# Moving a residual kernel's twelve data slots to the front of SBUF, at a multiple of 4096 bytes

## The chip, the cores and the metric

The kernel runs on one core of a Trainium2 chip. The metric is device time in microseconds (us) for one execution. Three runs of the kernel before took 325.68 to 326.02 us, with a median of 325.93 us. Times of single instructions and of stretches come from one profiled execution of the same kernel.

## The reference

There are 128 samples. Each has a matrix of 128 channels by 1024 time steps, and an index that names one of 8 subjects. Each subject has a 128 x 128 weight matrix. The output is the input plus the input multiplied by its subject's weights, all in float32:

```python
def reference(x, itok_B_0_7, L0_cond_weights):
    # x (128, 128, 1024), itok_B_0_7 (128,), L0_cond_weights (8, 128, 128)
    w = L0_cond_weights[itok_B_0_7]
    return x + jnp.einsum("bct,bcd->bdt", x, w)
```

One sample is 512 KB, so 67.1 MB are read and 67.1 MB are written, beside 0.5 MB of weights.

## The kernel before

The 128 samples are treated in 32 tiles of four samples, and a tile in two halves of two samples (`G = 2`, `H = 2`). A tile lives in one of 12 slots `x0` to `x11` in SBUF (line 95). A slot has 16384 bytes in each of the 128 partitions, four rows of 4096 bytes, one row for each sample. Tile `i` uses slot `i % 12`. A sample is loaded into its row, the sum is written over it, and the row is stored from there.

Loads are issued on ScalarE's queue, one of 512 KB for each sample (`load`, line 128). On the side of the input, four channels at a time form one run of 16384 bytes (`ROWS = 4`); on the side of SBUF, each channel is a row of 4096 bytes in its own partition. From the thirteenth tile on, ScalarE waits until the tile that had the slot has been stored.

Stores are issued on SyncE's queue (`store`, line 137), as a rule one of 2 MB for each tile, after both halves are summed. On the side of SBUF a run is the two neighbouring rows of a half, 8192 bytes; on the side of the output it is one row of 4096 bytes. Sample 0 goes by itself: it has its own load semaphore, product, sum and store, and so does sample 1 after it (line 229 on, `if j == 0`); their stores are 512 KB each, with runs of 4096 bytes. The second half of tile 0 and the first half of the last tile are stored as 1 MB, and the last two samples by themselves.

For each half tile `j`, GpSimd reads the subjects' indices, waits until the half has been loaded and copies the two subjects' weights from `w_all` into two of four buffers `ws` (line 210). TensorE then multiplies, four matmuls of 512 columns for each sample in two passes (line 223), into one of two PSUM tiles. VectorE adds the product to the slot's rows (line 242, and line 235 for sample 0). Before the first product TensorE multiplies zeros three times (line 155).

All of this is written in a fixed order for each engine; no planner decides it. The addresses of the tiles follow the order in which `sbuf(...)` is called (lines 89 to 95): first the four index rows, then all weights, the four weight buffers and the zeros, and the 12 slots last. What the language sets aside at the start of each partition ends at byte 16512. So the index rows begin there, and slot 0 at 26752.

Of the kernel before, what the change touches and what calls it, by code (L numbers as in the profile page):

```python
# [30 lines left out]
G = 2  # L31
H = 2
# [3 lines left out]
SLOTS = 12  # L36
# [8 lines left out]

ROWS = 4

PACE = 2
QUEUES = {mybir.EngineType.SP: "qSPDynamicHW", mybir.EngineType.Activation: "qActDynamicHW"}

# [22 lines left out]
def kernel(  # L73
# [7 lines left out]
    nc = tc.nc  # L81
    B, C, T = x.shape
# [3 lines left out]
    def sbuf(name, *shape, dtype=F32):  # L86
        return ctx.enter_context(nc.sbuf_tensor(name, list(shape), dtype)).ap()

    given, near, wrap, index = (
        sbuf(name, 1, B, dtype=I32) for name in ("given", "near", "wrap", "index")  # L90
    )
    w_all = sbuf("w_all", C, S, D)
    ws = [sbuf(f"w{i}", C, 1, D) for i in range(W_SLOTS)]
    zeros = sbuf("zeros", C, N)
    xs = [sbuf(f"x{i}", C, H * G, T) for i in range(SLOTS)]
    ps = [
        ctx.enter_context(nc.psum_tensor(f"ps{i}", [D, G, T], F32)).ap() for i in range(P_SLOTS)
    ]
# [19 lines left out]
    def emptied(i, h):  # L118

        turns = i // SLOTS  # L120
        return (DMA * G + (DMA if h == H - 1 else 0)) * turns - (DMA if i >= SLOTS and i % SLOTS == 0 and h == 0 else 0)
# [26 lines left out]
    with tc.tile_critical():  # L148
# [22 lines left out]
        for i in range(NT):  # L171
# [4 lines left out]
            if i >= SLOTS:  # L176
                nc.scalar.wait_ge(s_pair[k][H - 1], emptied(i, H - 1))
            if i == PACE:
                nc.scalar.wait_ge(s_one_issued, 1)
# [4 lines left out]
        for j in range(NT * H):  # L184
            i, q0, q1 = j // H, j % H * G, (j % H + 1) * G
# [105 lines left out]
```

## Time and profile before

| | |
|---|---|
| median of three runs | 325.93 us (325.68 to 326.02) |
| profiled execution | 325.98 us |
| its span, first to last instruction | 324.2 us |
| mean granted TensorE clock | 0.925 |
| TensorE matmul busy | 241.9 us (75%) |
| VectorE busy | 148.0 us (46%) |
| GpSimd busy | 34.3 us (11%) |
| moved by DMA | 134.85 MB in 16218 packets, mean 416 GB/s |
| load of one sample, issue to landing | 32.1 us (median of 128) |
| store of one tile, issue to landing | 47.0 us (median of 30) |

The span runs from the first instruction to the last; what the execution takes beyond it, 1.8 us here, lies around it. Busy shares are means over the span. DMA issues are not counted as busy time of the engine that issues them. A packet in the DMA rows is one run on the reading side, or a 4-byte write to a semaphore; 16 DMA engines work at the same time, and shares are of their time together.

### The profile page before, as it was taken

To read this page: it belongs to the slowest core of one execution; us is meant where nothing else is said; L and a number is where in the kernel's file an instruction comes from. 1 tells how busy PE (TensorE), PEld (TensorE's weight loads), DVE (VectorE), ACT (ScalarE), POOL (GpSimd) and SP (SyncE) were. 2 spreads that over 40 slices of the span, in tenths; PEclk is the share of its full clock that TensorE was granted. 3 is DMA by queue.
4 is the path that set the end of the run, shared out by engine and by line. 5 is a ranking of instruction groups with operands and counts; after the bars stand their busy time and mean duration, and the time that the engine had idled before them with its cause. 6 is when DMAs were issued, how large, how long until landed. Compare 5 with 4: busy or idle time off the path is not lost.

```text
span 324.2 us, 1611 instructions
## 1 busy us (share of the span) xinstructions
PE 241.9 (75%) x518; PEld 94.9 (29%) x518; DVE 148.0 (46%) x69; POOL 34.3 (11%) x132
## 2 busy tenths in 40 slices
PE   7999888888888888898888888888888769000000
PEld 3444333333333333333333333333333324000000
DVE  1566554555555554555555555555554552200000
POOL 1011110111111111111111111111111010000000
PEclk9999999999999999999999999999999997755555
DMA  7999999999999999999999999999999999999996
GB/s 259 395 427 429 422 425 423 427 428 424 427 426 425 426 418 430 427 420 432 423 422 426 424 426 421 428 422 426 428 428 419 424 428 424 427 423 429 427 427 255
DMA packets 16218, 134.85 MB, mean 416 GB/s; under 512 B 2641, under 2 KB 3666, under 8 KB 4178
## 3 DMA queue, kind: packets, MB, share of 16 engines
q10 hardware_dynamic: 7184, 67.64, 49.9%
q1 hardware_dynamic: 9026, 67.11, 49.3%
q8 instruction: 4, 0.07, 0.1%
q14 instruction: 4, 0.03, 0.0%
HBM read 67.63 MB, written 67.11 MB: 416 GB/s over the span
## 4 chain that ended last, share of the span: by engine, by line
PE 40%; DVE 21%; issue 17%; POOL 4%; DMA 2%; POOLq 1%; ACTq 1%; SPq 0%
PE ps L223 40%; DVE x L242 21%; POOL w L210 4%; DMA x<-in_x_dram 2%; POOLq L210 1%; ACTq L59 1%; ACTq L170 0%; ACTq L287 0%; SPq L148 0%
## 5 line engine op out<-in xcount | busy, mean ns | idle before, releaser
L223 PE MATMUL ps<-x,w 128*128 128x512 f32 x512 | 236.9, 608 | 32.8 <-POOL w L210 32.5
L242 DVE TENSOR_TENSOR x<-ps,x 128x2048 f32<-128x2048 f32 (+1 forms) x64 | 145.6, 2275 | 123.1 <-PE ps L223 123.1
L223 PEld LDWEIGHTS ps<-x,w 128*128 128x128 f32 x512 | 93.0, 191 | 176.9 <-issue 93.2
L210 POOL COPY w<-w_all 128x128 f32 x128 | 34.1, 296 | 237.3 <-DMA x<-in_x_dram 223.6
L155 PE MATMUL ps<-zeros 128*128 128x512 f32 x6 | 4.9, 990 | 1.7 <-DVE zeros L152 1.7
L235 DVE TENSOR_TENSOR x<-ps,x 128x1024 f32<-128x1024 f32 x1 | 1.2, 1224 | 5.7 <-PE ps L223 5.7
L155 PEld LDWEIGHTS ps<-zeros 128*128 128x128 f32 x6 | 1.8, 328 | 3.7 <-issue 2.1
L152 DVE MEMSET zeros<- 128x512 f32 x1 | 0.5, 485 | 1.1 <-SPq L148 1.1
L162 DVE TENSOR_SCALAR near<-given 1x128 int32<-1x128 int32 x1 | 0.2, 214 | 0.6 <-DMA given<-in_itok_B_dram 0.6
L166 DVE CUSTOM_DVE_ANT_0 index<-near,wrap 1x256 uint16<-1x256 uint16 x1 | 0.3, 280 | 0.0
L164 DVE TENSOR_SCALAR wrap<-near 1x128 int32<-1x128 int32 x1 | 0.2, 216 | 0.0
L278 POOL MEMSET const-float32-0.0<- 128x1 f32 x1 | 0.1, 99 | 0.2 <-issue 0.2
L278 POOL MEMSET const-bfloat16-1.0<- 128x1 bf16 x1 | 0.1, 102 | 0.0
L278 POOL MEMSET const-uint8-127<- 128x1 uint8 x1 | 0.1, 102 | 0.0
L278 POOL MEMSET const-float32-1.0<- 128x1 f32 x1 | 0.1, 99 | 0.0
## 6 DMA issues: line engine op xcount, KB each, us to landing
x<-in_x_dram ACTq DMA_DIRECT2D x128, 512.0 KB, 32.1
out_dram<-x SPq DMA_DIRECT2D x30, 2048.0 KB, 47.0
out_dram<-x SPq DMA_DIRECT2D x4, 512.0 KB, 16.3
out_dram<-x SPq DMA_DIRECT2D x2, 1024.0 KB, 20.4
w_all<-in_L_cond_weights_dram ACTq DMA_DIRECT2D x1, 512.0 KB, 4.3
given<-in_itok_B_dram SPq DMA_DIRECT2D x1, 0.5 KB
```

What stands on the lines that cost most here:

```text
L59: return engine.add_instruction(mybir.InstDMACopy(name=nc.get_next_instruction_name(), engine=engine.engine, ins=ins, outs=outs, mode="Cop ...
L152: nc.vector.memset(zeros, 0.0).then_inc(s_zeros, 1)
L155: nc.tensor.matmul(ps[P_SLOTS - 1][:, G - 1, :N], zeros[:, :D], zeros, start=True, stop=True)
L162: nc.vector.tensor_scalar(near, given, -S, S - 1, ALU.max, ALU.min).then_inc(s_index, 1)
L164: nc.vector.tensor_scalar(wrap, near, 0, S, ALU.is_lt, ALU.mult).then_inc(s_index, 1)
L166: nc.vector.tensor_tensor(index, near, wrap, ALU.add).then_inc(s_index, 1)
L210: copy = nc.gpsimd.tensor_copy(ws[b % W_SLOTS], w_all[:, bass.ds(subject[b % R], 1), :])
L223: mm = nc.tensor.matmul(p[:, q % G, t : t + N], ws[(i * H * G + q) % W_SLOTS][:, 0, :], xs[k][:, q, t : t + N], start=True, stop=True,)
L235: nc.vector.tensor_tensor(one, p[:, 0, :], one, ALU.add).then_inc(s_one_added, 1)
L242: nc.vector.tensor_tensor(mine, p[:, q0 % G :, :], mine, ALU.add).then_inc(s_added, 1)
L278: nc = _bacc.Bacc("TRN2", target_bir_lowering=False, num_devices=1)
```

## The change

The 12 slots are allocated first, ahead of all other tiles. Before them stands a tile `room` that nothing uses. Its size is what is missing from the first free byte to the next multiple of 4096: 3968 bytes, from 16512 to 20480. Slot 0 then begins at byte 20480, which is 5 x 4096, and slot `k` at 20480 + 16384 `k`. The index rows, the weights, the weight buffers and the zeros follow after the last slot, from byte 217088 on. Before, slot 0 began at 26752, which is 128 past a multiple of 256 and 2176 past a multiple of 4096. Instructions, queues, waits and sizes of transfers are the same, in the same order on each engine.

```diff
 ROWS = 4
+
+ALIGN = 4096
...
+    room = -(nc.sbuf_base + -nc.sbuf_base % 32) % ALIGN
+    if room:
+        sbuf("room", C, room // 4)
+    xs = [sbuf(f"x{i}", C, H * G, T) for i in range(SLOTS)]
     given, near, wrap, index = (
         sbuf(name, 1, B, dtype=I32) for name in ("given", "near", "wrap", "index")
     )
     w_all = sbuf("w_all", C, S, D)
     ws = [sbuf(f"w{i}", C, 1, D) for i in range(W_SLOTS)]
     zeros = sbuf("zeros", C, N)
-    xs = [sbuf(f"x{i}", C, H * G, T) for i in range(SLOTS)]
```

## The prediction

> **What bounds the kernel now.** I read the page's utilisation slices first, then its DMA queues, then the waits, and last single stretches of the run.
>
> The slices (40 equal parts of the span: busy tenths of the DMA engines, then GB/s) and the queues (packets, MB, share of the time of 16 DMA engines):
>
> ```profile
> span 324.2 us, 1611 instructions
> DMA  7999999999999999999999999999999999999996
> GB/s 259 395 427 429 422 425 423 427 428 424 427 426 425 426 418 430 427 420 432 423 422 426 424 426 421 428 422 426 428 428 419 424 428 424 427 423 429 427 427 255
> q10 hardware_dynamic: 7184, 67.64, 49.9%
> q1 hardware_dynamic: 9026, 67.11, 49.3%
> ```
>
> The 16 DMA engines are full from the second slice to the last but one, at a rate that hardly moves. Loads (q10) and stores (q1) together fill 99.2% of 16 engines' span. The waits (who waited for whom: us, times, longest) show the compute engines waiting for loads:
>
> ```profile
> POOL w L210 <- DMA x<-in_x_dram: 223.6, 59, 6.9
> DVE x L242 <- PE ps L223: 123.1, 64, 5.7
> SPq L59 <- DVE x L242: 225.4, 29, 12.2
> ```
>
> The chain of waits names PE for 40% of the span, but each of its pieces starts when GpSimd, which had waited for a load, copies a weight. I trust the waits: PE is busy 75% of the span, DVE 46%, and neither is at work at all in the last 40 us, while the DMA engines still run at the same 427 GB/s (busy time of each engine, granted clock, DMA share, GB/s):
>
> ```profile
> 60.00:260.00 200.00, 174.57 (x379) 67.78 (x378) 107.71 (x47) 25.05 (x94) 1.00 1.01 425
> 260.00:290.00 30.00, 13.17 (x26) 4.96 (x24) 9.17 (x4) 1.60 (x6) 0.76 1.01 426
> 290.00:310.00 20.00, 0.00 (x0) 0.00 (x0) 0.00 (x0) 0.00 (x0) 0.50 1.01 427
> ```
>
> So the time is the sum of packet times on one DMA engine. Only a change in what a packet costs can move it.
>
> **What a packet costs before.** A packet is one read run. A load is 32 packets of 16384 bytes (four rows of x), each written as four 4096-byte rows of a slot. A store of a half tile or more is packets of 8192 bytes read from a slot and written as two 4096-byte rows of the output; a store of one sample is packets of 4096 bytes. Two stretches give the means (queue rows of 50 to 100 us, then of 290 to 300 us, stores alone):
>
> ```profile
> q10 hardware_dynamic: 1141, 12.45, 59.0%
> q1 hardware_dynamic: 1139, 8.81, 42.0%
> ...
> q1 hardware_dynamic: 554, 4.28, 101.6%
> ```
>
> First row: 59.0% of 16 x 50 us is 472.0 us; 12.45 MB are 760 load packets, the other 381 are 4-byte semaphore packets of 9 ns, so (472.0 - 3.4) / 760 = 617 ns. Second: (336.0 - 0.6) / 1075 = 312 ns. Third: (162.6 - 0.3) / 522 = 311 ns. Shares pass 100% because a packet's record overlaps the next one's by some ns, so what an engine pays is the distance from one start to the next, which I took from the trace's single packet records: 6 ns for 4 bytes, 23.5 for 512 (the weights), 155 for 4096, 306 to 307 for 8192, and for 16384 bytes 607 until about 30 to 35 us of the span and 613 from then on. Check: 38 loads x 607 + 218 x 613 + 496 stores x 307 + 32 x 155 + 64 x 23.5 + 165 x 6 ns = 316.4 us per engine; the rest of 324.2 us is the 2 us before the first packet, the slower start (307 GB/s over the first 12 us) and the last 1.5 us.
>
> **The change part by part.** The built programs give the addresses. Before, slot 0 lies at byte 26752 of each partition, 128 past a multiple of 256 and 2176 past one of 4096; slots are 16384 bytes and rows 4096, so every row of every slot has this remainder. After, slot 0 lies at 20480, remainder zero, and so all rows. Every engine issues the same instructions in the same order, with the same waits; nothing passes a queue.
>
> *The filler tile* (992 floats per partition) is never touched: nothing.
>
> *The small tiles* (index rows, weights, zeros) move from 16512 to 217088 and up. Their work is 128 weight copies of 296 ns, 9 other small instructions, and 64 packets per engine for the weights. The copies stand behind 223.6 us of waiting for loads, so even twice their 34.1 us would be covered; if that cover were gone, each half tile would wait another 0.6 us. The weight packets are in the DMA sum: between 0 and 64 x 4.7 ns = 0.3 us less. I take 0.
>
> *The slots* carry 256 load packets and 528 store packets per engine, all on the path. No row has a slot packet at remainder zero, so I bound it. Top of the gain: everything that a packet costs beyond its bytes goes. A line through the two load sizes, (607 - 23.5) / (16384 - 512) = 0.03676 ns per byte, leaves 4.7 ns per packet: 784 x 4.7 = 3.7 us. Bottom: the next slower values in the same records, 621 ns for some loads and 314 for some stores against the usual 616 and 311, for all: 256 x 5 + 496 x 3 = 2.8 us more. Between these I take zero, by the nearest row: the line from the loads gives 155.3 ns for 4096 bytes and 305.9 for 8192, and stores were seen at 155 and 306. Loads read aligned HBM rows and write offset slots, stores read offset slots; a charge for the one would not be the charge for the other. The 4-byte semaphore packets, which touch no slot, pay as much (6 - 0.1).
>
> The page "DMA: Bandwidth & Descriptors" of the Trainium skill, section "How a descriptor splits into AXI transactions", says otherwise: a transaction "must start from a 256B-aligned address", and bytes fetched before the start cost beats. By that rule each store packet now fetches 128 bytes too many, and my sum would end at 323.4 us, as the second rival does; by the rows it stays. That 4096-byte stores are on the loads' line speaks against it, but no run here has yet shown a store from an aligned slot.
>
> *Sum*: 0 us. The profiled execution took 325.98 us (324.2 of span and 1.8 around it), the median of three runs is 325.93, so the two bases agree and I forecast **325.9 us**. About 0.2%, 0.65 us, is what a measurement of this kernel can tell from no change.
>
> **The rivals.**
>
> *The late surcharge goes.* From 30 to 35 us on, each load packet costs 613 instead of 607 ns, and most store packets 307 instead of 306. If broken rows are what makes packets of the two queues hold each other up, aligned ones would keep the early values: 218 x 6 + about 430 x 1 = 1.7 us, 324.2 us. For it: a constant surcharge on nearly every packet is what a fixed property of addresses would give. Against it: the first 34 to 39 loads of every engine had the same offset and many ran between stores without it, so something else changed after some 19 samples.
>
> *Offset stores pay for the half block that they don't need.* 128 bytes x 0.03676 = 4.7 ns for each of 528 store packets: 2.5 us, 323.4 us. If the 4.7 ns of every packet were such a price, loads too, it would be the 3.7 us above, 322.2 us. For it: the extra 4.7 ns of a store packet is of just that size. Against it: the loads and the semaphore packets pay the same.
>
> *Slower: aligned rows collide.* With all rows beginning at the same low address bits, the slots' packets on 16 engines might meet in the same part of the memory more often, and then take the slower values of the records: 2.8 us more, 328.7 us at the worst. It decides from 0.65 us / 784 = 0.8 ns per packet, between 20 and 322 us of the span, since nothing idles there that could take it up. Against it: all rows have one common remainder mod 4096 already, and the change only makes it zero. What could also go is that compute slows; with PE at 174.57 of 200 us in the steady stretch it would need 15% longer matmuls.
>
> That the change doesn't move the slots is excluded by the addresses.
>
> **How the numbers follow.** No change 0.46 (325.3 to 326.6 us). Late surcharge gone 0.19 (324.2, partly gone up to 325.3). Half blocks saved 0.15 (323.4, with 0.03 of it near 322.2). Slower 0.20 (326.6 to 328.7). Faster is 0.34. The range of 323.2 to 327.8 us leaves out the lowest 0.03 to 0.05 and the upper half of the slower case, about 0.1; the likeliest case's own range is 325.3 to 326.6.
>
> **What would show it.** Right: load packets at a mean of about 617 ns and stores at 311 to 312 in the same stretches, 425 to 427 GB/s in the slices. Late surcharge gone: 611 ns loads throughout, 311 turning into 309, some 428 GB/s between 50 and 250 us. Half blocks: the pure store stretch at 306 ns and above 430 GB/s, loads as before. Slower: that stretch or the mixed one below 424 GB/s, at the same packet counts. I would be wrong above all if the 4.7 ns of a store packet, which I count as the price of any packet, is two things of the same size.

## The result: 0.9 us faster, and where it lies

The changed kernel took 325.00 us (median of eight runs, 324.72 to 325.26), the kernel before 325.93 us (325.51 to 326.03). The ratio is 0.9975, with a 95% interval of 0.9964 to 0.9986. So it is faster by 0.9 us, a quarter of a per cent: nearly twice the whole spread of the kernel before (0.5 us), and far less than a glance at a profile shows.

The page of the changed kernel: utilisation slices (40 parts of the span) and the two DMA queues (packets, MB, share of 16 engines' time).

```profile
span 323.4 us, 1611 instructions
DMA  7999999999999999999999999999999999999996
GB/s 241 409 429 431 423 426 425 429 424 426 428 428 424 428 423 424 429 425 428 424 431 425 422 430 422 426 425 433 424 427 423 423 432 423 426 424 428 429 423 274
q10 hardware_dynamic: 7184, 67.64, 50.0%
q1 hardware_dynamic: 9026, 67.11, 49.3%
```

The DMA engines are as full as before, with the same packets and the same bytes; the span is 0.8 us shorter. The waits (us, times, longest) have kept their order and nearly their size, since compute still waits for loads:

```profile
POOL w L216 <- DMA x<-in_x_dram: 220.3, 58, 7.1
DVE x L248 <- PE ps L229: 121.6, 64, 5.4
```

The same three stretches as before the change, by windows (busy us of PE, PEld, DVE and POOL with the number of instructions, granted clock, DMA share, GB/s):

```profile
60.00:260.00 200.00, 174.82 (x377) 67.97 (x376) 107.67 (x47) 24.90 (x95) 0.99 1.01 426
260.00:290.00 30.00, 12.83 (x28) 4.88 (x26) 9.17 (x4) 1.57 (x6) 0.78 1.01 427
290.00:310.00 20.00, 0.00 (x0) 0.00 (x0) 0.00 (x0) 0.00 (x0) 0.50 1.01 427
```

From 60 to 260 us, where loads and stores are both at work, the rate went from 425 to 426 GB/s; from 290 to 310 us, where stores run alone, it is 427 as before. One unit of rounding is all that these rows show of the gain. The queue rows of one such stretch show more. From 100 to 200 us, of the kernel before and then of the changed one:

```profile
q10 hardware_dynamic: 2281, 24.91, 59.0%
q1 hardware_dynamic: 2281, 17.51, 41.8%
```

```profile
q10 hardware_dynamic: 2284, 24.97, 59.2%
q1 hardware_dynamic: 2282, 17.52, 41.6%
```

In q1, 17.51 MB are 2137 packets of 8192 bytes, and 41.8% of 16 x 100 us, less 1.3 us of semaphore packets, gives 312.3 ns for each. After the change it is (665.6 - 1.3) / 2139 = 310.6 ns. Loads moved by less than these roundings tell.

The single packet records tell it sharply. Before, store packets of 8192 bytes had records of 309 and 311 ns, and besides 846 of 312, 381 of 313 and 482 of 314 ns; 1900 of 7936 lay above 311. After, 18 do. All but 7 of the 1900 had lain in the time in which loads ran too, which ends at 270 us; from 290 to 310 us there was none before either. The mean from 50 to 250 us of the span fell from 312.0 to 310.56 ns for stores and from 616.5 to 616.2 ns for loads.

### The profile page after: what moved, and what is told of

Read it like the earlier page. It is cut to its first block, busy times and chain, and to the rows that moved or that the text cites. A ratio compares the mean times of both kernels' runs of the same rounds, so it can differ in the third digit from the quotient of the medians.

```text
span 323.4 us, 1611 instructions
## 1 busy us (share of the span) xinstructions
PE 241.5 (75%) x518; PEld 94.9 (29%) x518; DVE 148.0 (46%) x69; POOL 34.0 (11%) x132
## 4 chain that ended last, share of the span: by engine, by line
PE 40%; DVE 21%; issue 16%; POOL 4%; DMA 2%; POOLq 1%; ACTq 1%; SPq 0%
PE ps L229 40%; DVE x L248 21%; POOL w L216 4%; DMA x<-in_x_dram 2%; POOLq L216 1%; ACTq L61 1%; ACTq L176 0%; ACTq L293 0%; SPq L154 0%
## 6 DMA issues: line engine op xcount, KB each, us to landing
out_dram<-x SPq DMA_DIRECT2D x30, 2048.0 KB, 46.4
```

## The experiments

Every comparison is with the kernel before, run on the same chip between the others. "Slow stores" below are store packets of 8192 bytes with a record above 311 ns. The expectation of e1 gives their number as 1898 before and 24 after the change; the traces have 1900 and 18.

### Place or remainder: e1, e2, e3, e4

Two things were changed at once: slots come first, and they begin at a multiple of 4096. Four kernels take them apart. One leaves the slots last and fills up to 28672:

```diff
+ALIGN = 4096
...
 w_all = sbuf("w_all", C, S, D)
 ws = [sbuf(f"w{i}", C, 1, D) for i in range(W_SLOTS)]
 zeros = sbuf("zeros", C, N)
+room = -(nc.sbuf_base + -nc.sbuf_base % 32) % ALIGN
+if room:
+    sbuf("room", C, room // 4)
 xs = [sbuf(f"x{i}", C, H * G, T) for i in range(SLOTS)]
```

> The slots stay behind the small tiles as before, but begin at byte 28672, a multiple of 4096. If the remainder of the rows' addresses is what counts (mod 256 or mod 4096), the ratio to before is about 0.9975 as for the changed kernel, and store packets of 8192 bytes with a record above 311 ns are nearly gone (24 of 7936 in the changed kernel, 1898 before). If the place of the slots or of the small tiles is what counts, the ratio is 1.000 and about 1900 such records stay.

Measured: 0.9967 (0.9955 to 0.9979), 33 slow stores. The next two are the changed kernel with another filler, which puts slot 0 at 2176 past a multiple of 4096 (e2) or, with 256 in place of 2176, at 256 past one (e3):

```diff
-    room = -(nc.sbuf_base + -nc.sbuf_base % 32) % ALIGN
+    room = (2176 - (nc.sbuf_base + -nc.sbuf_base % 32)) % ALIGN
```

> The slots come first, but begin at byte 18560, 2176 past a multiple of 4096 and 128 past one of 256, as in the kernel before. By either rule of remainders the ratio is 1.000 and about 1900 store packets lie above 311 ns; if the order of the tiles counts, the ratio is 0.9975 and they are nearly gone.

Measured: 0.9999 (0.9990 to 1.0008), 1978 slow stores.

> The slots come first and begin at byte 16640, a multiple of 256 that is 256 past a multiple of 4096. If only the remainder mod 256 counts, the ratio is 0.9975 and slow store packets are nearly gone. If rows must not cross a multiple of 4096, the ratio is 1.000 and about 1900 stay.

Measured: 0.9978 (0.9969 to 0.9987), 76 slow stores. The changed kernel itself was run beside them:

> The changed kernel again, beside the other three on one chip. If its gain is the remainder's, the ratio is 0.9975 within 0.001. If the gain came from the runs' spread, it goes back to within 0.0005 of 1.

Measured: 0.9972 (0.9963 to 0.9981), 36 slow stores.

So the place of the slots and of the small tiles is worth nothing that these runs show, and a multiple of 4096 is not needed: a multiple of 256 does the same. Run anew, the changed kernel has its gain again, of the same size.

### Loads' writes or stores' reads: e5, e6, e7, e8

A slot is written by a load and read by a store, at the same address. To tell the two apart, VectorE wrote its sum 128 or 256 bytes ahead of the input. Each slot is 256 bytes longer, and VectorE's addition waits for its own previous one, since it overwrites the tail of the rows before. For e5:

```diff
-    xs = [sbuf(f"x{i}", C, H * G, T) for i in range(SLOTS)]
+    both = [sbuf(f"x{i}", C, H * G * T + 64) for i in range(SLOTS)]
+    xs = [b[:, 32 : 32 + H * G * T].rearrange("c (q t) -> c q t", t=T) for b in both]
+    ys = [b[:, : H * G * T].rearrange("c (q t) -> c q t", t=T) for b in both]
...
-    mine, p[:, q0 % G :, :], mine, ALU.add
+    ys[k][:, q0:q1, :], p[:, q0 % G :, :], mine, ALU.add
```

and the stores read `ys`. The three others differ in the slots' start and in the shift.

> VectorE writes the sum 128 bytes ahead of where the input was loaded: loads write rows that begin 128 past a multiple of 256, stores read from multiples of 256. If the stores' reads from offset rows are what costs, the ratio is about 0.9975 and store packets above 311 ns are nearly gone (under 100 of 7936). If the loads' writes to offset rows are what costs, the ratio is 1.000 and about 1900 stay.

Measured: 1.0002 (0.9993 to 1.0012), 2135 slow stores.

> The mirror image: loads write to multiples of 256, stores read 128 past one. If the stores' reads cost, the ratio is 1.000 and about 1900 store packets lie above 311 ns; if the loads' writes cost, 0.9975 and under 100.

Measured: 0.9971 (0.9959 to 0.9982), 7 slow stores.

> Control of the other two: the sum is written 256 bytes ahead of the input, both begin at multiples of 256. The ratio is 0.9975 and under 100 slow store packets by either theory; another ratio would be the price of the shifted write and its one wait on VectorE.

Measured: 0.9980 (0.9970 to 0.9989), 22 slow stores.

> Control: the sum is written 256 bytes ahead, both begin 128 past a multiple of 256. The ratio is 1.000 and about 1900 slow store packets by either theory. If loads and stores each cost about half, the two mixed kernels lie at 0.9988 with some 900 slow packets each.

Measured: 1.0003 (0.9994 to 1.0012), 2117 slow stores.

The two mixed kernels side by side, by windows in the stretch where both queues work (e5 first, then e6):

```profile
60.00:260.00 200.00, 175.46 (x381) 68.25 (x380) 108.27 (x48) 24.87 (x94) 1.00 1.01 425
```

```profile
60.00:260.00 200.00, 176.34 (x379) 68.50 (x378) 109.31 (x48) 24.87 (x94) 0.99 1.01 426
```

The result is clear, and I had not expected it this way round: the store packets are slow when the *loads* write to offset rows. Where stores read from makes no difference that these runs show. In e6 every store reads 128 past a multiple of 256, as before the change, and the whole gain is there. The charge of an offset write thus shows in the record of a packet of the other queue.

TensorE and VectorE read the rows where the loads wrote them, so these four kernels move their reads together with the loads' writes. The start of the run tells the two apart in part, since the first store packet comes only at some 14 us. Of the loads that had ended by then, 100 of 223 have records of 618 to 660 ns in the kernel before, and 15 of 220 in the changed one, where most have 611. It is so in every profiled execution: 67 to 175 of some 210 to 240 in the seven kernels whose loads write off a multiple of 256 (95 in e5), 5 to 22 in the seven whose loads write at one (22 in e6). Before the first product, when no engine had read a slot yet, it is 20 of 27 loads before the change and 1 of 25 after, though some offset kernels show none there (0 of 16 in e11). So an offset write can be slow with neither a store nor a compute engine beside it. What the reads of the compute engines add in the mixed stretch, if anything, no run shows.

### How the price depends on the remainder: e9, e10, e11

The filler was set so that rows begin 32 and 224 bytes past a multiple of 256. For 16, which the allocation does not give by itself, the slots are a slice of one long tile:

```diff
-    xs = [sbuf(f"x{i}", C, H * G, T) for i in range(SLOTS)]
+    line = sbuf("line", C, SLOTS * H * G * T + 64)[:, 4 : 4 + SLOTS * H * G * T]
+    line = line.rearrange("c (i q t) -> c i q t", i=SLOTS, t=T)
+    xs = [line[:, i] for i in range(SLOTS)]
```

> Rows begin 32 bytes past a multiple of 256 (slot 0 at 20512). If any remainder mod 256 costs the load one broken piece at each end of a row, the ratio is 1.000 and about 2000 store packets lie above 311 ns, as for 128. If the cost grows with the remainder, or with the smaller piece, it is a quarter or so: 0.998 and about 500.

Measured: 1.0071 (1.0058 to 1.0084), 328.12 us, 4285 slow stores.

> Rows begin 224 bytes past a multiple of 256, the mirror image of 32. One broken piece at each end: 1.000 and about 2000 slow store packets. Cost in proportion to the bytes before the start: slower than before, 1.002. Cost by the smaller piece: as for 32.

Measured: 1.0065 (1.0052 to 1.0078), 327.92 us, 4283 slow stores.

> Rows begin 16 bytes past a multiple of 256, so that no 32-byte unit of a row is whole in memory. If only the broken 256-byte blocks count, 1.000 and about 2000 slow store packets. If a smaller unit of 32 bytes is written in one step, each row takes one unit more (32 bytes x 0.0368 = 1.2 ns): 4 x 256 rows, 1.2 us, and 1.004.

Measured: 1.0111 (1.0096 to 1.0126), 329.28 us, 4317 slow stores.

None of the expectations for 32 and 224 held: the price is neither that of 128 nor in proportion to the remainder, it is three to four times that of 128, counted from aligned rows, and the same for 32 as for 224. Only that likeness of 32 and 224 stood among the expectations. For 16 bytes the direction of the second expectation held (1.004 was worked out, 1.011 came). The profile shows it without any single records now. Windows of e9 and then of e11, in the mixed stretch and with stores alone:

```profile
60.00:260.00 200.00, 171.85 (x372) 66.68 (x371) 107.70 (x47) 24.88 (x94) 1.00 1.01 421
290.00:310.00 20.00, 0.00 (x0) 0.00 (x0) 0.00 (x0) 0.00 (x0) 0.50 1.01 426
```

```profile
60.00:260.00 200.00, 171.85 (x372) 66.50 (x370) 106.71 (x47) 24.61 (x93) 1.00 1.01 419
290.00:310.00 20.00, 0.00 (x0) 0.00 (x0) 0.00 (x0) 0.00 (x0) 0.50 1.02 427
```

421 and 419 GB/s against 426 with aligned rows, but 426 to 427 as soon as the loads have ended. Below are the means of the packet records, in ns, from 50 to 250 us (mixed) and from 290 to 310 us (stores alone) of the profiled executions:

```
loads write at   stores read at   kernel    store, mixed   load, mixed   store, alone
(bytes past a multiple of 256)
  0                0              changed       310.56        616.23        310.87
  0              128              e6            310.55        616.22        310.88
128                0              e5            311.87        616.92        310.88
128              128              before        312.00        616.53        310.88
 32               32              e9            315.69        620.82        310.87
224              224              e10           315.76        620.84        310.88
 16               16              e11           316.83        624.60        310.87
```

The last column does not know of any remainder. The two before it go by the first column, within 0.2 ns for stores and 0.4 ns for loads.

### Fewer, longer store packets: e12

If a packet costs 4.7 ns beyond its bytes, longer packets should save time on top of alignment. A store of a whole tile was read in runs of four rows:

```diff
-            xs[k][:, q0:q1, :].rearrange("d (o g) t -> d o (g t)", g=min(G, q1 - q0)),
+            xs[k][:, q0:q1, :].rearrange("d (o g) t -> d o (g t)", g=q1 - q0),
```

> The changed kernel with stores of a whole tile read in runs of 16384 bytes instead of 8192: 240 packets per engine fewer. If each packet costs 4.7 ns beyond its bytes and nothing is lost elsewhere, 1.1 us less than the changed kernel: ratio to before 0.994. If longer store packets make the loads wait as much longer, 0.9975 stays; the other 0.9 ns per packet that 8192-byte packets cost in the mixed stretch may go as well.

Measured: 325.63 us, 0.9993 (0.9984 to 1.0001), with a wide spread of 324.27 to 326.05 us: neither 0.994 nor 0.9975. The packets' records did shrink, from 321.1 to 319.5 us per engine, and the time did not follow. Queues of e12 from 100 to 200 us, its whole-tile stores after those of the changed kernel (number, KB, median us from issue to landing), and its end by windows:

```profile
q10 hardware_dynamic: 1963, 21.40, 50.7%
q1 hardware_dynamic: 1455, 21.22, 50.0%
```

```profile
out_dram<-x SPq DMA_DIRECT2D x30, 2048.0 KB, 46.4
out_dram<-x SPq DMA_DIRECT2D x30, 2048.0 KB, 13.5
```

```profile
290.00:310.00 20.00, 15.15 (x34) 5.87 (x33) 9.17 (x4) 2.12 (x8) 1.00 1.00 422
310.00:323.80 13.80, 5.02 (x12) 1.69 (x10) 4.58 (x2) 0.53 (x2) 0.86 0.74 309
```

In the mixed stretch the 4.7 ns were not there to be saved: from one start to the next, a store packet of 16384 bytes most often takes 613 ns, and two of 8192 take 614. From 20 to 115 MB moved, e12 is 0.2 us ahead of the changed kernel. It loses at the end. In the changed kernel the two queues take turns by packet: 2284 and 2282 from 100 to 200 us, semaphore writes counted, and loads had 24.97 of 42.5 MB. In e12 a store's turn moves twice the bytes, and the store queue keeps running out of work: it has 1455 packets against 1963, and a whole tile has landed 13.5 us after its issue, not 46.4. Loads and stores then move the same bytes (21.40 and 21.22 MB), as I read it because a tile can be stored only once it has been loaded. So the loads end late, at 311 us instead of 270: PE still works 15.15 us of the stretch from 290 to 310 us, where in the changed kernel it had nothing left to do, and the last products, sums and stores stand at the end with nothing beside them. In the last 13.8 us the DMA engines move 309 GB/s, against 335 in the last 13.8 us of the changed kernel; the way from 132 to 134 MB takes 6.7 us instead of 4.7. The shorter packets in the store queue are what lets the loads run ahead. No run beat the changed kernel by more than the intervals; e1 and e6, at 0.9967 and 0.9971, do the same with less or other rearrangement.

## Why the prediction was right and where it was wrong

**What bounds the kernel.** This held. The differences seen between the other kernels, from -1.1 to +3.5 us, go with what packets cost, and PE's stretches only follow; e12 alone lost its time at the end.

**The forecast of no change.** It missed by 0.9 us: 325.0 lies in the wide range and outside 325.3 to 326.6, the range of the likeliest case. That the wide range holds it is owed to the room left for rivals, not to the mechanism that was forecast. The step that failed is the slots' term, "Between these I take zero, by the nearest row". The line went through starts 607 ns apart for loads and 23.5 for weights, and was checked with store packets at 155 and 306: values of packets that nothing disturbs. They do lie on one line, and they are the same after the change, so the base price of a packet was read rightly. But the time is made of packets in the mixed stretch, and there a row of the kernel before already held the price: the mean store record was 312, not the 309 or 311 that an undisturbed one takes. I had seen 314 ns in those records and used them as the end for a loss, though they were what could be gained. Worked out from the measured means: some 359 store packets of 8192 bytes per engine lie in the mixed time (496 less the 42 us after the last loads at 0.307 us each), at 1.45 ns, and 256 loads at 0.3 ns, together 0.6 us. The traces bear out most of that. From 20 MB moved (some 51 us) to 115 MB (some 274 us, when the loads have just ended), the six profiled executions with aligned loads and stores of 8192 bytes take 223.28 to 223.31 us, and the four whose loads write at 128, the kernel before among them, take 223.75 to 223.81: 0.5 us, with hardly any scatter. The medians differ by 0.7 to 1.1 us. The rest lies before 20 MB and after 115 MB, where profiles of one kind differ by 0.3 to 0.4 us among themselves; it isn't settled. The start held a sign too: the check of the packet costs took 607 ns for all loads of the first 30 us, but 100 of the 223 ahead of the first store had records of 618 to 660 ns.

**The late surcharge.** The idea in it, that broken rows make the packets of the two queues hold each other up, came nearest: writes to broken rows do cost, though not only where the two queues meet. What it named is not what went: loads still cost 613 ns from some 35 us on, start to start, and 607 before, with aligned rows too. What sets in at that time stays open.

**The half blocks of offset reads.** Refuted. Stores alone have records of 310.87 or 310.88 ns, and start 307 ns apart, whether they begin 0, 128, 32, 224 or 16 bytes past a multiple of 256, and e6 has the whole gain with offset reads. The rule of the Trainium skill, page "DMA: Bandwidth & Descriptors", section "How a descriptor splits into AXI transactions", that bytes before an offset start are fetched and cost beats, is thus not seen for reads from SBUF: 224 bytes would be 8.2 ns for each store packet at 0.0368 ns per byte, and 0.0 was measured. What counts here is the loads' writes.

**Aligned rows collide.** Refuted: the three kernels whose rows begin at multiples of 4096, with slot 0 at 20480 (twice) and at 28672, are all faster than before.

**What would show it.** Stores alone stayed at 311 ns and 427 GB/s, as said for no change. The rate in the mixed stretch moved by one unit, too little for the row that I had named.

How an offset write comes to cost time stays open. It does not need stores beside it, as the start of the runs shows, and not every offset write pays: with 16 bytes of offset, 142 load packets still have the record of 611 ns that most have in aligned kernels before the first store. Why 32, 224 and 16 cost more than 128 is open too; no run here lies between 32 and 128.

## What to carry to other kernels

Where DMA is the bound, let the rows that loads write in SBUF begin at a multiple of 256 bytes. In this kernel that is worth 0.3% against 128 past it, 1.0% against 32 or 224 past it and 1.4% against 16 past it, and costs a filler of at most 224 bytes. The source of a store needs no such care. Read a packet's price in the stretch in which the time is spent, as a mean with its tail, and not from the most frequent value: 24% of the stores were a few ns slow, and the mixed stretch in which they lay holds about half of the change.

## What was unexpected in the hardware

Where both queues work, the delay that an offset write causes shows in packets of the other queue as well: with loads at 128, load records grew by 0.3 to 0.7 ns, and store records by 1.3 to 1.5 ns. The step from 128 to 32 bytes of remainder is larger than the one from 0 to 128 (store records 310.6, 312.0, 315.7 ns; loads 616.2, 616.5, 620.8). And while both have work, two queues on the same DMA engines share by packets, not by bytes: 2284 and 2282 in 100 us, 4-byte semaphore writes counted as packets. Store packets of 16384 instead of 8192 bytes took the loads from 59% of the bytes to 50% and moved the end of compute from 277 to 319 us, at the same 426 GB/s from 60 to 260 us.
